# Graph attention in two layers: where an attention block's output projection stands in the order of work

## The chip, the cores and the metric

The kernel runs on one core of one Trainium2 chip. The metric is device time in microseconds (us) of one execution, lower is better. Five engines run their own instruction queues beside each other: PE (TensorE, the matmuls), DVE (VectorE), ACT (ScalarE), POOL (GpSimd) and SP (SyncE, which here issues the DMAs). They wait for one another through semaphores.

## What is computed

The input is x of 8 elements, 2048 nodes and 256 features, with one adjacency matrix of 2048 x 2048 for all elements. Everything is in 32-bit floats. Two layers follow each other, cut here to what matters:

```
# layer 0: masked attention, 4 heads of 64, softmax apart over each chunk of 256 keys
scores = clip(q @ k.T / 8, -10, 10);  scores[adj == 0] = -10
attn   = softmax over the 256 keys of each of 8 chunks
ctx    = sum over chunks of attn @ v
out    = ctx @ Wo.T + bo + x
x      = layernorm(x + (layernorm(out) * gamma + beta))
# layer 1: graph attention
Wh     = x @ W;  e = leaky_relu(Wh @ a1 (rows) + Wh @ a2 (columns));  e[not adj] = -inf
h      = elu(softmax(e) @ Wh)
x      = layernorm(x + h)
```

## The kernel before, in words

Layer 0 works in blocks of 512 queries, named (b,ib): element b of 8, block ib of 4. A block passes over 8 chunks of 256 keys. Each chunk takes two **beats**, so there are 512 beats with attention in them, and a block has 16. The order of all instructions is written out by hand, and each engine executes its own in that order.

One beat, in the order in which it is written:

1. `begin_beat` (lines 816 to 834), for layer 1: exponentials of the edge weights that are ready (`weights`, ACT, with a sum on POOL), the next edge steps' linear part (`low`, ACT, line 714), and `leaky` on DVE (line 718) for the steps begun in the beat before.
2. Scores: four matmuls of 512 columns on PE (line 899) into two tiles of PSUM, two clips and caps on DVE (line 909), two exponentials on ACT (line 912).
3. `middle_of_beat` (line 914): `edges`, the masks of layer 1, on DVE (line 723).
4. Values of the chunk before (line 928). In the first beat of a chunk, which is even, two parts: the denominators (part 2) and the first half of the values (part 0). In the second beat, which is odd, the other half (part 1). Each part takes one PSUM tile of the pool `ps_m`, which has two buffers, and ACT copies it out (lines 936 and 942).
5. `end_beat` (lines 842 to 856): the products of layer 1 on PE (line 746), then one step of each generator in `ahead` (the preludes of layer 1) and `fins` (projections of keys and values, the block ends, and so on), then what is due in `agenda`, such as the scaling of a chunk's values and its addition to the context `ctxT` (DVE line 963, POOL line 964).

Layer 1 may begin an edge step 1.5 times per beat, which gives two and one in turn. A step passes `low`, `leaky` and `edges`, then `weights` and its product two beats after it began.

The generator `fin` (line 343) ends a block of layer 0. It loads x, prepares `y` = x + bo on POOL, and waits until the last chunk has been added to `ctxT`. It goes on in the beat after that, which is an odd one. Then, in one beat, it writes the output projection (two tiles `po` of pool `ps_m`, 8 matmuls in all at line 357, each added to `y` on DVE at line 364) and the statistics of the first normalization. In the following beats come the normalization (ACT), gamma and beta (POOL), the statistics of the second one, its normalization with the store `h_d` and the count `fin_near`, and the transposes `pt` (line 383) with the store `hT_d`. The prelude of element b in layer 1 begins when `fin_near` shows all four blocks; it makes Wh (`pw`), the masked maxima (`fb`, line 438), the rows `pab` (line 461), and then layer 1's steps can begin. All of `po`, `pt`, `pw`, `pab`, and the projections `pq`, `pk`, `pv` share the two buffers of `ps_m` with the values.

The first product of a layer-1 block writes the one PSUM tile `us`, which ACT must have copied out for the block before it (line 773).

Of the kernel before, what the change touches and what calls it, by code (L numbers as in the profile page):

```python
# [9 lines left out]
F32 = mybir.dt.float32  # L10
# [9 lines left out]
P = 128  # L20
# [8 lines left out]
def tile_adj_attention__then__gat(  # L29
# [35 lines left out]
    nc = tc.nc  # L65
    B, N, F = x.shape
    H, D = 4, 64
    CHUNK = 256
    KC = F // P
    NT = N // P  # L70
    IB = 512
    NIB = N // IB
    TPB = IB // P
# [12 lines left out]
    ps_m = ctx.enter_context(tc.tile_pool(name="ps_m", bufs=2, space=PSUM))  # L86
# [21 lines left out]
    def load_w(name, w):  # L108
        t = const.tile([P, KC, F], F32, name=f"WT_{name}")
        nc.sync.dma_start(out=t, in_=w.rearrange("(k p) o -> p k o", p=P))  # L110
        return t
# [11 lines left out]
    WT = {"k": load_w("k", WkT)}  # L123
# [187 lines left out]
    def stats(src, name):  # L311

        st = two.tile([P, TPB, 6], F32, tag="st", name=f"st_{name}")
        mv = two.tile([P, TPB, 2], F32, tag="mv", name=f"mv_{name}")
        for t in range(TPB):
            nc.vector.bn_stats(st[:, t, :], src[:, t, :])
            nc.vector.bn_aggr(mv[:, t, :], st[:, t, :])
            if t == TPB // 2 - 1 and beat < 2 * NIB * NCH:
                yield
        rstd = two.tile([P, TPB], F32, tag="rstd", name=f"rstd_{name}")  # L320
        nc.vector.tensor_scalar_add(rstd, mv[:, :, 1], EPS)
        nc.gpsimd.tensor_tensor(rstd, rstd, nhalf, ALU.pow)
        return mv, rstd

    def normalize(dst, mv, rstd, name):
        nmr = two.tile([P, TPB], F32, tag="nmr", name=f"nmr_{name}")
        nc.vector.scalar_tensor_tensor(nmr, mv[:, :, 0], -1.0, rstd, ALU.mult, ALU.mult)
        for t in range(TPB):
            nc.scalar.activation(
                dst[:, t, :], dst[:, t, :], AF.Identity, bias=nmr[:, t : t + 1], scale=rstd[:, t : t + 1]  # L330
            )

    def bc_rows(v):
        return v.unsqueeze(1).to_broadcast([P, TPB, F])
# [2 lines left out]
    hT_d = dram.tile([B, NIB, P, KC, IB], F32, name="hT_d")  # L337
    fin_near = [0] * B
    ctx_done = {}
    fins = []  # L340

    def fin(b, ib, ctxT):


        xt = one.tile([P, TPB, F], F32, tag="x", name=f"x{b}_{ib}")
        nc.sync.dma_start(out=xt, in_=x[b, ts(ib, IB), :].rearrange("(t p) f -> p t f", p=P))
        yield
        y = one.tile([P, TPB, F], F32, tag="y", name=f"y{b}_{ib}")
        nc.gpsimd.tensor_add(y, xt, bc_rows(bo_bc))  # L349
        nc.gpsimd.tensor_add(xt, xt, bc_rows(beta_bc))  # L350
        while (b, ib) not in ctx_done or ctx_done[b, ib] == beat:
            yield
        for t2 in range(TPB // 2):
            po = ps_m.tile([P, 2, F], F32, tag="m", name=f"po{b}_{ib}_{t2}")
            for j in range(2):
                for k in range(KC):
                    nc.tensor.matmul(  # L357
                        po[:, j, :],
                        ctxT[:, k, ts(2 * t2 + j, P)],
                        WT["o"][:, k, :],  # L360
                        start=(k == 0),
                        stop=(k == KC - 1),
                    )
            nc.vector.tensor_add(y[:, ts(t2, 2), :], po, y[:, ts(t2, 2), :])
        mv, rstd = yield from stats(y, f"a{b}_{ib}")
        yield
        normalize(y, mv, rstd, f"a{b}_{ib}")
        yield
        engine = nc.vector if (b, ib) == (B - 1, NIB - 1) else nc.gpsimd
        engine.tensor_mul(y, y, bc_rows(gamma_bc))  # L370
        engine.tensor_add(y, y, xt)
        yield
        mv, rstd = yield from stats(y, f"b{b}_{ib}")
        yield
        normalize(y, mv, rstd, f"b{b}_{ib}")
        nc.sync.dma_start(out=h_d[b, ib], in_=y)
        fin_near[b] += 1
        yield
        hT = four.tile([P, KC, IB], F32, tag="xT", name=f"hT{b}_{ib}")
        for k in range(KC):  # L380
            pt = ps_m.tile([P, TPB, P], F32, tag="m", name=f"pt{b}_{ib}_{k}")
            for t in range(TPB):
                nc.tensor.transpose(pt[:, t, :], y[:, t, ts(k, P)], ident)
            nc.scalar.copy(hT[:, k, :], pt.rearrange("p t c -> p (t c)"))
        if (b, ib) == (B - 1, NIB - 1):
            states[b]["hT"] = hT
        else:
            nc.sync.dma_start(out=hT_d[b, ib], in_=hT)
# [447 lines left out]
    def middle_of_beat():  # L836
        nonlocal edged
        for s in leaking:
            s.edges()
        edged = leaking  # L840
# [32 lines left out]
    for J in range(total + 1):  # L873
        b, ib, j = J // (NIB * NCH), J // NCH % NIB, J % NCH
        live = J < total
        if live and j == 0:
            ctxT = one.tile([P, 2, IB], F32, tag="ctx", name=f"ctxT{b}_{ib}")
        cur = {"b": b, "ib": ib, "j": j, "es": [], "ctxT": ctxT, "v": vs[min(b, B - 1)], "name": f"{b}_{ib}_{j}"}
        for half in range(2):
# [14 lines left out]
            if live:  # L894
                scs = []
                for hp in range(NPAIR):
                    sc = ps_s.tile([P, 2, IB], F32, tag="sc", name=f"sc{b}_{ib}_{c}_{hp}")
                    for h in range(2):
# [4 lines left out]
                            start=True,  # L903
                            stop=True,
# [5 lines left out]
                for hp in range(NPAIR):  # L910
                    e = eight.tile([P, 2, IB], F32, tag="e", name=f"e{b}_{ib}_{c}_{hp}")
                    nc.scalar.activation(e, scs[hp], AF.Exp)  # L912
                    cur["es"].append(e)
            middle_of_beat()

            early = J < NIB * NCH
            if prev is not None:
                if half == 0:

                    pool, tag = (one, "hr") if early and J % 3 == 2 else (two, "un")  # L920
                    prev["un"] = pool.tile([P, 2, IB], F32, tag=tag, name=f"un{prev['name']}")
                for part in ((2, 0), (1,))[half]:
                    m = ps_m.tile([P, IB], F32, tag="m", name=f"u{prev['name']}_{part}")
                    for i in range(2):
                        pc = 2 * prev["j"] + i
                        for h in range(H):
# [5 lines left out]
                                start=(i == 0),  # L932
                                stop=(i == 1),
# [3 lines left out]
                    else:  # L937
# [20 lines left out]
                        def scaled(p=prev):  # L958
                            r2 = p["r"].unsqueeze(1).to_broadcast([P, 2, IB])
                            if p["j"] == 0:  # L960
                                nc.vector.tensor_mul(p["ctxT"], p["un"], r2)
                            else:
                                nc.vector.tensor_mul(p["un"], p["un"], r2)  # L963
                                nc.gpsimd.tensor_add(p["ctxT"], p["ctxT"], p["un"])  # L964
                            if p["j"] == NCH - 1:
                                ctx_done[p["b"], p["ib"]] = beat
                            if p["j"] == NCH - 3:
                                fins.append(fin(p["b"], p["ib"], p["ctxT"]))
# [66 lines left out]
```

## Time and profile before

| what | value |
|---|---|
| time, median of 3 runs | 4400.04 us (4389.66 to 4401.98) |
| the profiled execution's own time | 4387.29 us |
| its span | 4385.5 us |
| mean granted clock of TensorE | 0.98 |
| DVE, scores clipped, L909 | 1024 x 1223 ns |
| PE, scores, L899 | 4096 records, 1060.4 us |
| PE, values and denominators, L928 | 980.9 and 497.5 us |
| PE, products of layer 1, L746 | 878.6 us |
| PE, output projection, L357 | 512 records, 120.2 us |
| DVE, sum of projection and y, L364 | 64 x 689 ns |

Each program matmul in 32-bit floats shows as two or four records. In the lines of groups, waits and timelines, `a<-b` reads "writes a from b", L is the line of the kernel, and the bracket at the end of a timeline line is the time that the engine stood idle before it, with what ended the wait. PEld is the load of weights into PE, which overlaps matmuls.

### The profile page before, as it was taken

What the parts mean: (1) busy time and instruction counts of PE and PEld (TensorE: products, weight loads), DVE (VectorE), ACT (ScalarE), POOL (GpSimd) and SP (SyncE); (2) the same over time, 40 slices, a digit from 0 to 9 for tenths busy, and PEclk for the clock granted to TensorE, in tenths of its full rate; (3) what the DMA queues carried; (4) which work ended last, traced back from release to release, by engine and by line L of the source; (5) the groups of instructions that cost most, each with busy time, mean ns of one, the idle gap of its engine ahead of it and who ended that gap; (6) DMA issues with size and microseconds to landing.
All of it is one profiled execution on the core that took longest, in us unless ns stands there. A gap on an engine that the chain in (4) does not pass through costs nothing. (4 is left out here: it accounts for less than half of the span.)

```text
span 4385.5 us, 61171 instructions
## 1 busy us (share of the span) xinstructions
PE 4064.2 (93%) x23053; PEld 1907.6 (43%) x23053; DVE 3417.7 (78%) x4530; ACT 2564.4 (58%) x3842; POOL 1760.5 (40%) x901
## 2 busy tenths in 40 slices
PE   8889989999999999999899999999999999899767
PEld 3223334454344534454344543445434454344456
DVE  5876589965998669976699766996579965888777
ACT  5655556665566556666566665566556665555546
POOL 0222235543455334444245442554325542354420
PEclk9999999999999999999999999999999999999889
DMA  5554232222332233321333223232232222322321
GB/s 166 182 163 149 71 115 86 83 73 89 99 90 81 64 107 102 100 75 51 105 102 98 74 74 105 85 95 78 70 106 85 89 78 67 115 83 80 123 73 58
DMA packets 257641, 415.63 MB, mean 95 GB/s; under 512 B 85440, under 2 KB 120512, under 8 KB 256448
## 3 DMA queue, kind: packets, MB, share of 16 engines
q1 hardware_dynamic: 257344, 411.71, 30.5%
q8 instruction: 181, 2.97, 0.3%
q14 instruction: 116, 0.95, 0.1%
HBM read 340.66 MB, written 68.88 MB: 93 GB/s over the span
## 5 line engine op out<-in xcount | busy, mean ns | idle before, releaser
L912 ACT ACTIVATE e<-sc 128x1024 f32<-128x1024 f32 x1024 | 1034.2, 1020 | 1049.9 <-DVE sc L909 1006.7
L909 DVE SCALAR_TENSOR_TENSOR sc<-sc,mk 128x1024 f32<-128x1024 f32 x1024 | 1206.7, 1223 | 538.3 <-PE sc L899 352.6
L899 PE MATMUL sc<-qT,kT 64*128 64x512 f32 x4096 | 1060.4, 633 | 86.7 <-ACT e L912 86.2
L964 POOL TENSOR_TENSOR ctxT<-ctxT,un 128x1024 f32<-128x1024 f32 x224 | 568.5, 2538 | 1145.3 <-DVE un L963 1007.0
L928 PE MATMUL u<-e,v 128*32 128x512 f32 x8192 | 980.9, 597 | 0.0
L746 PE MATMUL us<-wh,w 128*128 128x256 f32 x3584 | 878.6, 395 | 81.9 <-ACT w L727 60.4
L746 PEld LDWEIGHTS us<-wh,w 128*128 128x128 f32 x3584 | 667.7, 193 | 422.2 <-ACT w L727 110.7
L736 POOL TENSOR_TENSOR acc<-acc,w 128x512 f32<-128x512 f32 x392 | 601.7, 1535 | 544.9 <-ACT w L727 534.4
L899 PEld LDWEIGHTS sc<-qT,kT 64*128 64x128 f32 x4096 | 347.2, 189 | 611.6 <-ACT e L912 281.8
L718 DVE SCALAR_TENSOR_TENSOR w<-ab,sj,w 128x512 f32<-128x512 f32 x512 | 571.5, 1137 | 4.6 <-ACT w L714 4.5
L928 PEld LDWEIGHTS u<-e,v 128*32 128x32 f32 x8192 | 240.6, 110 | 659.7 <-issue 543.9
L928 PE MATMUL u<-e,ones 128*32 128x512 f32 x4096 | 497.5, 604 | 0.0
L723 DVE TENSOR_TENSOR w<-w,mk 128x512 f32<-128x512 f32 x512 | 458.6, 917 | 37.1 <-DMA mk<-mask 34.6
L438 DVE CUSTOM_DVE_ANT_0 fb<-sj_row,fb 128x1024 bf16<-128x1024 f32 x240 | 387.8, 1626 | 2.3 <-DMA fb<-far 2.3
L714 ACT ACTIVATE w<-ab,sj 128x512 f32<-128x512 f32 x512 | 352.2, 714 | 8.7 <-POOL acc L734 5.4
L727 ACT ACTIVATE w<-w 128x512 f32<-128x512 f32 x512 | 308.8, 629 | 75.9 <-DVE w L723 75.3
L936 ACT COPY un<-u 128x512 f32<-128x512 f32 x512 | 300.5, 587 | 66.5 <-PE u L928 57.6
L963 DVE TENSOR_TENSOR un<-un,r 128x1024 f32<-128x1024 f32 x224 | 278.1, 1242 | 42.2 <-DMA r<-rd 36.7
L928 PEld LDWEIGHTS u<-e,ones 128*32 128x32 f32 x4096 | 107.8, 110 | 356.5 <-issue 305.4
L950 DVE RECIPROCAL dc<-dc 128x16 f32<-128x16 f32 x256 | 63.9, 249 | 149.8 <-DMA dc<-ds 134.0
L942 ACT COPY ds<-u 128x512 f32<-128x512 f32 x256 | 148.5, 580 | 3.0 <-PE u L928 2.5
L349 POOL TENSOR_TENSOR y<-x,bo_bc 128x1024 f32<-128x1024 f32 x32 | 77.6, 2426 | 163.6 <-DMA x<-in_x_dram 103.0
(112 smaller groups left out, 3114.7 us busy)
## 6 DMA issues: line engine op xcount, KB each, us to landing
r<-rd SPq DMA_DIRECT2D x256, 256.0 KB
mk<-mask SPq DMA_DIRECT2D x120, 512.0 KB
fb<-far SPq DMA_DIRECT2D x240, 256.0 KB
xT_k<-in_xT_dram SPq DMA_DIRECT2D x32, 512.0 KB
raw<-in_adjT_dram SPq DMA_DIRECT2D x32, 512.0 KB
rawf<-in_adj_dram SPq DMA_DIRECT2D x32, 512.0 KB
x<-in_x_dram SPq DMA_DIRECT2D x32, 512.0 KB
h_d<-y SPq DMA_DIRECT2D x32, 512.0 KB
```

Source lines behind the costliest of these rows:

```text
L438: nc.vector.tensor_tensor_reduce(out=fb, in0=row, in1=fb, scale=1.0, scalar=2 * FAR * 0.999, op0=ALU.add, op1=ALU.max, accum_out=dst,)
L714: nc.scalar.activation(self.w, k["ab"][:, 1, :], AF.Identity, bias=k["sj"][:, 1, c : c + 1])
L718: nc.vector.scalar_tensor_tensor(self.w, k["ab"][:, 0, :], k["sj"][:, 0, c : c + 1], self.w, ALU.add, ALU.max)
L723: nc.vector.tensor_tensor(self.w, self.w, self.k["mks"][self.c // HT][:, self.c % HT, :], ALU.min)
L727: nc.scalar.activation(self.w, self.w, AF.Exp)
L736: nc.gpsimd.tensor_add(k["acc"], k["acc"], self.w)
L746: nc.tensor.matmul(k["us"][:, t, :], self.w[:, ts(t, P)], k["wh"][c // TPB][:, c % TPB, 0:F], start=(first and t % 2 == 0), stop=last, ski ...
L899: nc.tensor.matmul(sc[:, h, :], kTs[b][c // TPB][h * D : (h + 1) * D, hp, ts(c % TPB, P)], qT[h * D : (h + 1) * D, hp, :], start=True, sto ...
L909: nc.vector.scalar_tensor_tensor(scs[hp], scs[hp], -CLIP, cap, ALU.max, ALU.min)
L912: nc.scalar.activation(e, scs[hp], AF.Exp)
L928: nc.tensor.matmul(m[h * DH : (h + 1) * DH, :], prev["v"][pc // TPB][:, pc % TPB, f0 : f0 + DH] if part < 2 else ones[:, 0:DH], prev["es"] ...
L964: nc.gpsimd.tensor_add(p["ctxT"], p["ctxT"], p["un"])
```

## The change

The projection's code becomes a function. For all blocks but the last of the last two elements, (6,3) and (7,3), `fin` puts that function into a list, and the list is emptied in the next beat's middle: after the scores and `edges` of that beat, and before its values. For those two blocks it is called at once, as before. `fin` yields after having put it there, so what follows in `fin`, from the statistics on, is written one beat later for the 30 blocks.

```diff
@@ -337,6 +337,7 @@
     ctx_done = {}
+    middle = []
     fins = []
@@ -350,18 +351,27 @@
         while (b, ib) not in ctx_done or ctx_done[b, ib] == beat:
             yield
-        for t2 in range(TPB // 2):
-            po = ps_m.tile([P, 2, F], F32, tag="m", name=f"po{b}_{ib}_{t2}")
...
-            nc.vector.tensor_add(y[:, ts(t2, 2), :], po, y[:, ts(t2, 2), :])
+
+        def output_projection():
+            for t2 in range(TPB // 2):
+                po = ps_m.tile([P, 2, F], F32, tag="m", name=f"po{b}_{ib}_{t2}")
+                for j in range(2):
+                    for k in range(KC):
+                        nc.tensor.matmul(
+                            po[:, j, :],
+                            ctxT[:, k, ts(2 * t2 + j, P)],
+                            WT["o"][:, k, :],
+                            start=(k == 0),
+                            stop=(k == KC - 1),
+                        )
+                nc.vector.tensor_add(y[:, ts(t2, 2), :], po, y[:, ts(t2, 2), :])
+
+        if b < B - 2 or ib < NIB - 1:
+            middle.append(output_projection)
+            yield
+        else:
+            output_projection()
         mv, rstd = yield from stats(y, f"a{b}_{ib}")
@@ -912,6 +922,8 @@
             middle_of_beat()
+            while middle:
+                middle.pop(0)()
```

More of the change, by code (lines that the diff above doesn't have):

```diff
@@ L352, in fin @@
             yield
-        for t2 in range(TPB // 2):
-            po = ps_m.tile([P, 2, F], F32, tag="m", name=f"po{b}_{ib}_{t2}")
[L355 to L364, printed above, removed]
+        def output_projection():
[16 more added lines that the diff above has]
+            output_projection()
         mv, rstd = yield from stats(y, f"a{b}_{ib}")
```

## The prediction

> **What bounds the kernel now.** Read in this order: busy times, who PE waited for, the output projection's tile `po`, then the timelines of PE and DVE around one projection. The waits' columns are total us, times, longest.
>
> ```profile
> PE 4064.2 (93%) x23053; PEld 1907.6 (43%) x23053; DVE 3417.7 (78%) x4530; ACT 2564.4 (58%) x3842; POOL 1760.5 (40%) x901
> ...
> PE sc L899 <- ACT e L912: 86.2, 57, 6.3
> PE us L746 <- ACT w L727: 60.4, 43, 10.8
> PE us L746 <- ACT hx L773: 21.5, 7, 3.9
> PE po L357 <- POOL ctxT L964: 16.4, 13, 2.6
> PE pab L461 <- ACT ds L942: 16.2, 18, 1.8
> ...
> PE pt L383 <- ACT ds L942: 14.4, 13, 1.8
> ...
>   DVE y L364: 61.8, 35
> ```
>
> PE is busy for 93% of the span. By windows, 82 us of its idle time lie after the last scores (276.7 less 195.1 busy from 4108.8 on); before, it idles some 25 us per element of attention (526.8 less 502.5 from 1084.6 to 1611.4), in short gaps. So a stall put into PE's order counts, and a gap filled counts. The last line says that DVE waits 61.8 us for `po`. That is mostly harmless, because DVE has slack in most stages. Block (2,1), PE first and then DVE:
>
> ```profile
> 1222.43 3.72 PE L746 MATMUL us<-wh,w 128*128 128x256 f32 x16
> 1225.99 3.61 PE L357 MATMUL po<-WT_o,ctxT 128*128 128x256 f32 x16
> 1229.53 1.99 PE L899 MATMUL sc<-qT,kT 64*128 64x512 f32 x8
> 1231.45 1.92 PE L928 MATMUL u<-e,ones 128*32 128x512 f32 x16
> 1233.19 1.90 PE L928 MATMUL u<-e,v 128*32 128x512 f32 x16
> ...
> 1246.28 2.43 PE L746 MATMUL us<-wh,w 128*128 128x256 f32 x8 [2.94 <-ACT hx L773]
> ```
> ```profile
> 1220.91 2.81 DVE L718 SCALAR_TENSOR_TENSOR w<-ab,sj,w 128x512 f32<-128x512 f32 x1
> 1223.65 2.35 DVE L909 SCALAR_TENSOR_TENSOR sc<-sc,mk 128x1024 f32<-128x1024 f32 x2
> 1225.91 0.84 DVE L723 TENSOR_TENSOR w<-w,mk 128x512 f32<-128x512 f32 x1
> 1226.68 1.21 DVE L438 CUSTOM_DVE_ANT_0 fb<-sj_row,fb 128x1024 bf16<-128x1024 f32 x1
> ...
> 1227.91 0.69 DVE L364 TENSOR_TENSOR y<-po,y 128x512 f32<-128x512 f32 x1
> 1229.64 0.69 DVE L364 TENSOR_TENSOR y<-po,y 128x512 f32<-128x512 f32 x1 [1.03 <-PE po L357]
> ...
> 1232.57 1.41 DVE L718 SCALAR_TENSOR_TENSOR w<-ab,sj,w 128x512 f32<-128x512 f32 x2
> 1233.90 2.36 DVE L909 SCALAR_TENSOR_TENSOR sc<-sc,mk 128x1024 f32<-128x1024 f32 x2
> ```
>
> PE runs without a gap here, and DVE is behind: it clips the scores of this beat 3 to 5 us after PE began them.
>
> **What the Trainium skill says.** "PSUM — Partial Sum Buffer", Engine vs sequencer instructions: the queues of ScalarE, VectorE and GpSimdE are strictly first in, first out, and matmuls complete in program order. The trace agrees: the second y above waits 1.03 us and everything of the next beat on DVE comes after it. "Perfetto Trace Analysis", Matmuls: independent groups should rotate through PSUM banks so that evacuating one overlaps the next. Here the pool `m` has two buffers for u, po, pk, pv, pw, pt and pab alike, and the pt and pab rows above are waits for a buffer of it. "SBUF — State Buffer", Who interferes with whom: a DVE instruction with two SBUF inputs contends with a GpSimd one that reads SBUF. L718 takes 0.66 us alone and 2.81 us above, so a DVE queue time has an error of some 2 us.
>
> **The change, part by part.** Call T the odd beat at whose end the projection stands now. It moves into beat T+1, after that beat's scores and before its values. No instruction is added: 16 po matmul records (3.6 to 3.7 us) and two y adds (1.4 us) per block, 30 of 32 blocks. No DMA is issued by the moved part itself. Everything after it in `fin` (bn statistics, both normalizations, gamma and beta, h_d store, transposes pt, hT_d store) comes one beat later, so these two stores stand one beat later on SP's queue. The h_d store then precedes an even beat's rd and r issues, where today the hT_d store does: an exchange, cost nothing; r is used two beats (about 15 us) after. Without that cover it costs the 2 us of one normalization.
>
> The new wait: values part 2 takes the buffer of po0, so it needs the first y add, which on DVE now stands behind leaky, two clips and edges of T+1. Behind the waiting matmul on PE stand all values and layer-1 products.
>
> A second consequence follows from the code. fin of (b,3), b up to 5, ends one beat later; the prelude of layer 1 waits for it, so layer 1 of elements 0 to 5 starts one beat later (beat T+23 of that block, not T+22). Layer 1 alternates two steps and one step per beat; starting on an even beat it is turned over: the beat with both value parts (3.7 us of u) now also gets two products (3.7 us), the odd one (1.9 us of u) gets one (2.0 us). PE's pair of beats stays at 4.0 + 5.6 + 5.6 = 15.2 us; DVE's too.
>
> Sums, against the profiled execution (span 4385.5, run 4387.3; the median of the runs shown is 4400.0, 0.3% above it):
>
> 1. Element 0 (no layer 1). (0,0) and (0,1) are DVE-bound; y waits of about 1.0 and 1.5 us go. (0,2): PE has no gap, 0. (0,3): PE stands 2.63 us before po; scores need only exp of T, some 2.3 us earlier than ctxT, then po, then values find y ready: 1.9 us. Sum -4.4.
> 2. (b,0), seven blocks: DVE-bound. The y wait of 0.84 us shrinks to about 0.3: -0.5 each, -3.5. The gap before po (1.87 us in (2,0)) doesn't go: scores of T+1 need exp of T, which is as late.
> 3. (b,1), b = 1 to 6. In (2,1), turned over, PE reaches the end of T's products at 1226.4, ends scores at 1228.4 and po at 1232.0. DVE, with leaky x2 (3.6 with one held up), ends T at 1228.0, then leaky 0.7, clips 2.35, edges 0.75, first y 0.7: 1232.6. Stall 0.6 us; with (7,1) about +4. If T's second leaky is held up too, 2 us more each.
> 4. (b,2), b = 1 to 6. fin1's statistics (2.3 us) now lie at T; DVE ends T at 1366.8, first y at 1371.4, po ended at 1369.1: stall 2.3. The gap of 1.3 for ctxT goes, because scores come first and ctxT is long done. +1.0 each, with (7,2) +6.5.
> 5. (b,3): DVE is idle 4.7 us there, y is ready before po ends: 0.
> 6. The first product of a new layer-1 block waits for the copy of `us` (the 2.94 us line; 21.5 us in 7). It moves from T+2 to T+3, behind 3.7 us of values and not 1.9, so about 1.3 remains: -1.6 x 6 = -9.6.
> 7. pt (14.4 us) waits for the ds copy, because it follows parts 2 and 0 of an even beat. One beat later it follows part 1 alone, whose buffer before last is long free. A quarter kept: -11.
> 8. pab in the same way, 0.42 and 0.90 us in each of six elements: -7.8.
>
> Total -25.8. Against that stands what the turn-over does in the 43 layer-1 beats of six elements, which no row shows. Between none of it and +35 us (a wait of the 0.34 or 0.56 us kind, L746 for L727, in half of the beats, less those that vanish). I take +8: where ACT and DVE are late, about a third of what PE recovers returns as another wait. Net -18 us: 4369 for the profiled execution, 4382 on the scale of the median. After the last scores nothing moves, since (6,3) and (7,3) are excepted.
>
> **Rivals.**
> - A, forecast, 0.57: short PE gaps close, 4382. For it: items 6 to 8 are repeated at the same place in each element.
> - B, given back, 0.18: the closed gaps return a beat later as waits for exp or for the new y, and only items 1 and 2 stay, 4400 - 4 = 4396. For it: DVE is idle only 5.3 us of the 135.9 in the window 1196.3 to 1332.2, which follows (2,1), so PE can't run ahead of it. Against it: at pt and pab the buffers are late on account of ACT's order, not of DVE's load.
> - C, slower, 0.25: values stall on the first y. It decides from where DVE gets to that add more than about 2 us after po ends on average. Were the turn-over not there, T+1 would have two leaky and two edges and (b,2) the maxima (3 us) before it: I get 2.1 us for (b,1) and 4.2 - 1.4 = 2.8 for (b,2), seven blocks each, 34 us; with one more hold-up of 2 us in half of these blocks 48, less items 1, 2 and half of 7 and 8: about +25, 4425 us. For it: 2.81 us leaky lines just at this place. Against it: DVE idle in (b,3) and no layer 1 in (b,0).
> - That nothing changes in the order is excluded: 30 blocks take the new branch.
>
> **How the numbers follow.** 4382 is A's. A's own range is 4355 to 4392, C reaches to 4440. From 4350 to 4420 about a tenth is left out at either end. About 0.3% (13 us) can be told from no change: A gives mostly faster, B same, C slower; 0.58, 0.17, 0.25.
>
> **What would show it.** Step 3 and 4: a new row, PE u waiting for DVE y, of 10 to 25 us in total. Over 50 us is C. Step 6: the hx row falls from 21.5 to about 12. Steps 7 and 8: the pt row near 4, pab near 8. Step 1: the po row for ctxT nearly gone in element 0. The turn-over: beats in (b,2) alternate about 9.4 and 5.9 us in place of 7.4 each; if they don't, the step on the prelude is wrong. The sc row for exp should stay near 86; if it grows by over 20, DVE is the bound and B or C holds.

## The result and the profile after

The changed kernel takes 4549.44 us (median of 4 runs, 4547.73 to 4553.29). The kernel before, measured beside it, takes 4399.95 us. The ratio is 1.0349, with a 95% interval of 1.0337 to 1.0362: slower by some 150 us, where the prediction said 18 us faster and a range up to 4420.

The profiled execution took 4548.56 us. Its span is 4546.7 us, 161.2 us longer than before, and its mean granted clock is 0.963 where it was 0.980. The busy times, from the page of the changed kernel:

```profile
PE 4131.4 (91%) x23053; PEld 1925.3 (42%) x23053; DVE 3493.0 (77%) x4530; ACT 2575.6 (57%) x3842; POOL 1761.9 (39%) x901
```

The same number of instructions keeps PE busy 67 us longer, and PE idles 94 us more (span less busy: 415.3 after, 321.3 before). The two add up to the 161 us. There are two things to explain: new gaps, and slower matmuls. In the lines below, `sc` are the scores, `e` their exponentials, `u` a chunk's values or denominators in PSUM, `un` and `ds` their copies, `w` the edge weights of layer 1, `us` its products and `hx` the copy of these. `dc`, `rd` and `r` are the denominators on their way: inverted, written to DRAM by one DMA, and spread over the partitions by the next. What PE waited for, from the view of its waits (total us, times, longest):

```profile
PE sc L909 <- ACT e L922: 179.2, 76, 6.3
PE us L756 <- ACT w L737: 56.1, 31, 10.8
PE pt L393 <- ACT un L948: 51.3, 23, 4.8
PE pw L408 <- ACT un L948: 21.9, 14, 4.9
PE u L940 <- DVE y L367: 19.2, 13, 1.6
...
PE us L756 <- ACT hx L783: 10.5, 7, 3.9
```

Scores now wait 93 us longer for exponentials (86.2 before), the transposes `pt` 37 us longer (14.4 before, for `ds`). The wait that the change was sure to add, values for the first add to `y`, is 19.2 us. The rows of `po` for `ctxT` (16.4) and of `pab` for `ds` (16.2) are gone.

The slower matmuls come with the gaps. Here are two places in the changed kernel's PE timeline, around scores that follow a gap (columns: start, length, operation, records, and in the bracket the idle time before):

```profile
1136.44 1.99 PE L909 MATMUL sc<-qT,kT 64*128 64x512 f32 x8
1138.36 1.92 PE L940 MATMUL u<-e,v 128*32 128x512 f32 x16
1145.76 3.52 PE L909 MATMUL sc<-qT,kT 64*128 64x512 f32 x8 [5.48 <-ACT e L922]
...
1067.29 1.11 PE L393 MATMUL pt<-ident,y 128*128 128x128 f32 x4 [2.87 <-ACT un L948]
1068.33 2.98 PE L909 MATMUL sc<-qT,kT 64*128 64x512 f32 x8
```

The same eight records take 1.99 us in a run without gaps, and 3.52 or 2.98 us behind a gap. The view by stretches of time shows why (second column the length, PEclk the one before the last two):

```profile
1142.00:1145.70 3.70, 0.00 (x0) 0.00 (x0) 3.58 (x5) 1.02 (x1) 2.34 (x1) 0.97 0.14 42
1145.70:1149.20 3.50, 3.44 (x8) 1.13 (x8) 3.50 (x6) 1.50 (x3) 0.00 (x0) 0.55 0.40 133
1149.20:1152.60 3.40, 3.40 (x18) 2.96 (x16) 1.93 (x2) 2.05 (x2) 0.00 (x0) 1.00 0.38 99
```

Behind the gap the granted clock is 0.55 for about 3.5 us and then full again. Summed over the clock records of the trace, TensorE stood at half clock for 342 us in 63 spells, against 180 us in 34 spells before; gaps of PE over 2 us number 61, and 37 before. Of 162 us more at half clock at most half is lost work, 81 us, which covers the 67. With the slower matmuls, the 94 us of gaps come to 161.

By block, as time from first scores to first scores of the next block: in elements 1 to 6 the (b,0) cost 36.0 us more in sum, the (b,1) 35.5, the (b,2) 47.6, the (b,3) 45.9. Element 0 costs 3.1 more, element 7 7.0 less. Layer 1 of an element runs beside the attention of the next one. The loss is thus spread over all of the time in which layer 1 runs, and is missing where there is none (element 0) or where it starts on its old beat (that of element 6, beside element 7).

### The profile page after: what moved, and what is told of

It is laid out like the page before. It is cut to its first block, busy times and chain, and to the rows that moved or that the text cites. A ratio compares the mean times of both kernels' runs of the same rounds, so it can differ in the third digit from the quotient of the medians.

```text
span 4546.7 us, 61091 instructions
## 1 busy us (share of the span) xinstructions
PE 4131.4 (91%) x23053; PEld 1925.3 (42%) x23053; DVE 3493.0 (77%) x4530; ACT 2575.6 (57%) x3842; POOL 1761.9 (39%) x901
## 5 line engine op out<-in xcount | busy, mean ns | idle before, releaser
L909 PE MATMUL sc<-qT,kT 64*128 64x512 f32 x4096 | 1105.8, 656 | 179.8 <-ACT e L922 179.2
L746 POOL TENSOR_TENSOR acc<-acc,w 128x512 f32<-128x512 f32 x392 | 583.6, 1489 | 724.3 <-ACT w L737 714.6
L909 PEld LDWEIGHTS sc<-qT,kT 64*128 64x128 f32 x4096 | 360.6, 195 | 725.2 <-ACT e L922 358.3
L728 DVE SCALAR_TENSOR_TENSOR w<-ab,sj,w 128x512 f32<-128x512 f32 x512 | 655.7, 1301 | 6.2 <-ACT w L724 6.1
L940 PE MATMUL u<-e,ones 128*32 128x512 f32 x4096 | 508.1, 615 | 19.2 <-DVE y L367 19.2
L733 DVE TENSOR_TENSOR w<-w,mk 128x512 f32<-128x512 f32 x512 | 417.5, 836 | 8.3 <-DMA mk<-mask 5.7
L975 DVE TENSOR_TENSOR un<-un,r 128x1024 f32<-128x1024 f32 x224 | 352.8, 1575 | 44.5 <-DMA r<-rd 44.3
L724 ACT ACTIVATE w<-ab,sj 128x512 f32<-128x512 f32 x512 | 352.3, 713 | 51.3 <-PE us L756 40.0
L448 DVE CUSTOM_DVE_ANT_0 fb<-sj_row,fb 128x1024 bf16<-128x1024 f32 x240 | 337.5, 1417 | 4.3 <-DMA fb<-far 4.1
L322 POOL TENSOR_TENSOR rstd_a<-rstd_a,nhalf 128x4 f32<-128x4 f32 x32 | 57.7, 1804 | 281.1 <-DVE rstd_a L321 218.2
```

The source lines that it names most:

```text
L448: nc.vector.tensor_tensor_reduce(out=fb, in0=row, in1=fb, scale=1.0, scalar=2 * FAR * 0.999, op0=ALU.add, op1=ALU.max, accum_out=dst,)
L724: nc.scalar.activation(self.w, k["ab"][:, 1, :], AF.Identity, bias=k["sj"][:, 1, c : c + 1])
L728: nc.vector.scalar_tensor_tensor(self.w, k["ab"][:, 0, :], k["sj"][:, 0, c : c + 1], self.w, ALU.add, ALU.max)
L733: nc.vector.tensor_tensor(self.w, self.w, self.k["mks"][self.c // HT][:, self.c % HT, :], ALU.min)
L746: nc.gpsimd.tensor_add(k["acc"], k["acc"], self.w)
L909: nc.tensor.matmul(sc[:, h, :], kTs[b][c // TPB][h * D : (h + 1) * D, hp, ts(c % TPB, P)], qT[h * D : (h + 1) * D, hp, :], start=True, sto ...
```

## The experiments

Each ratio is to the kernel before, run beside it on the same chip (medians 4389.2 to 4397.9 us in the five groups); 1% is 44 us. "Moved" means the projection in the middle of the next beat. e2 to e7, e9 to e11 and e14 to e16 ran twice each, the other experiments six times or more. The third and fourth columns say how many beats later than before layer 1's prelude and its steps are written, in elements 0 to 5.

| run | projection | prelude | steps | leaky | time us | ratio, 95% interval |
|---|---|---|---|---|---|---|
| the change | moved | +1 | +1 | ahead of clips | 4549.4 | 1.0349 [1.0337, 1.0362] |
| e1 | moved but for all (b,3) | 0 | 0 | ahead | 4413.3 | 1.0044 [1.0030, 1.0058] |
| e2 | old place | +1 | +1 | ahead | 4545.6 | 1.0349 [1.0324, 1.0374] |
| e3 | moved | 0 | 0 | ahead | 4436.6 | 1.0101 [1.0075, 1.0126] |
| e4 | old place, statistics a beat later | +1 | +1 | ahead | 4530.5 | 1.0314 [1.0289, 1.0339] |
| e5 | old place | +2 | +2 | ahead | 4474.8 | 1.0190 [1.0164, 1.0215] |
| e6 | old place | 0 | +1 | ahead | 4496.0 | 1.0238 [1.0218, 1.0258] |
| e7 | old place | +1 | +2 | ahead | 4435.7 | 1.0101 [1.0082, 1.0119] |
| e8 | moved in element 7 alone | 0 | 0 | ahead | 4383.6 | 0.9981 [0.9973, 0.9989] |
| e9 | moved | +1 | +1 | ahead | 4554.1 | 1.0376 [1.0331, 1.0420] |
| e10 | old place | 0 | +1 | ahead | 4486.7 | 1.0222 [1.0178, 1.0266] |
| e11 | moved | +1 | +1 | ahead | 4562.9 | 1.0396 [1.0351, 1.0441] |
| e12 | old place | 0 | +1 | behind clips | 4389.8 | 0.9989 [0.9980, 0.9998] |
| e13 | old place | 0 | 0 | behind | 4388.6 | 0.9990 [0.9982, 0.9998] |
| e14 | moved | +1 | +1 | behind | 4502.2 | 1.0246 [1.0205, 1.0288] |
| e15 | old place | +1 | +1 | behind | 4463.6 | 1.0155 [1.0117, 1.0193] |
| e16 | moved | 0 | +1 | behind | 4441.1 | 1.0104 [1.0061, 1.0146] |

### Is it the projection's place, or layer 1's later start? (e1 to e4)

Two theories stood after the first reading: the projection itself disturbs its beat (values behind the first `y` add, everything after it a beat late), or layer 1, which starts one beat later because `fin_near` is counted later, meets the attention's fixed work in another phase. e1 leaves the last block of every element in the old place, so that layer 1 keeps its beats:

```diff
-        if b < B - 2 or ib < NIB - 1:
+        if ib < NIB - 1:
```

> The change with (b,3) of every element left in its old place, so that 24 blocks are moved and layer 1 starts on the same beats as in the kernel before. Theory P (what costs is that layer 1 and its prelude start one beat later, on beats of the other parity): 4385 to 4430 us, half-clock time near the 180 us of before. Rival M (what costs is the moved projection itself, or the later rest of its block): about 24/30 of the loss stays, 4520 us. Rival V (values stall on the first y): loss in the rows of PE u waiting for DVE y, which would grow as T+1 has two leaky again, over 40 us in total.

e2 is the kernel before with nothing but one more `yield` ahead of the prelude:

```diff
+        if b < B - 2:
+            yield
```

> The kernel before, with one yield more in the prelude of layer 1 of elements 0 to 5; no projection is moved. Theory P: most of the loss without any moved projection, 4490 to 4550 us, and the clip of scores waiting on the spread of r as in the change. Rival M: 4400 us within 15.

e3 is the change with one `yield` less in the prelude, which puts layer 1 back on its beats:

```diff
-        yield
+        if b >= B - 2:
+            yield
```

> The change in full, with one yield fewer in the prelude of elements 0 to 5, so that layer 1 starts on the beats of the kernel before. Theory P: 4385 to 4430 us. Rival M: 4540 us, as the change.

e4 leaves the projection in its place and puts the extra `yield` of the 30 blocks behind it, ahead of the statistics:

```diff
             nc.vector.tensor_add(y[:, ts(t2, 2), :], po, y[:, ts(t2, 2), :])
+        if b < B - 2 or ib < NIB - 1:
+            yield
```

> The kernel before with the projection in its old place, but the rest of each block's end (statistics on) one beat later, for the 30 blocks. It keeps the later chain and the later start of layer 1, and drops the new place of the matmuls. Theory P, and a theory C (the later chain of each block costs): 4500 to 4560 us, as the change. If the place of the matmuls is what costs: 4400 to 4420.

e2 alone gives the whole ratio, 1.0349, without a moved projection. e1 and e3, with the projection moved and layer 1 on its old beats, cost 0.4 and 1.0%. e4, projection in the old place, costs 3.1%. So the later start of layer 1 is enough for the loss. The moved projection, with the end of its block a beat later, is a smaller loss by itself (44 us in e3), and it adds nothing to be seen when the other is there. By block, e3 loses most of it in (b,0), 25 us, where the transposes `pt`, a part of the later end, wait 22 us for `un`, and in (b,3), 20 us, where the values wait 21 us for `y` (sums over elements 1 to 6).

### The steps or the prelude, and does the phase come round? (e5 to e8)

e5 has two more `yield` ahead of the prelude in place of e2's one: layer 1 then has its two-step beats where they were, even or odd.

> The kernel before, with two yields more in the prelude of elements 0 to 5: layer 1 starts two beats later, on beats of the old parity. Theory P1 (parity): 4385 to 4415 us. Theory P2 (lateness, a beat of layer 1 is lost per element and has to be made up): at least the 150 us of the run with one yield, 4540 us or more.

e6 leaves the prelude on its beat and starts only the steps one beat later. e7 has e2's `yield` and this edit together: the prelude is one beat later and the steps two, so that beats with two steps are even or odd as before.

```diff
-            st["ab"][ib] = (beat + 2, query_bc(ab_d, f"{b}_{ib}"))
+            st["ab"][ib] = (beat + 2 + (b < B - 2), query_bc(ab_d, f"{b}_{ib}"))
```

> The kernel before, with the edge steps of layer 1 of elements 0 to 5 started one beat later by their due beat alone; the prelude's own work stays on its beats. Theory S (two products in the beat of two value parts, and what waits with them, cost): 4480 to 4545 us. Theory W (the prelude's own work, its loads, maxima and pw on beats of the other parity, costs): 4390 to 4415 us.

> The kernel before, with the prelude of elements 0 to 5 one beat later and the steps two beats later, so that the steps keep their parity and only the prelude's own work is turned over. Theory S: 4390 to 4420 us. Theory W: 4480 to 4545 us. If both have a share, this run's loss and that of the steps alone add up to about 150 us.

e8 moves the projection in element 7 alone, where the row by row comparison showed a gain:

```diff
-        if b < B - 2 or ib < NIB - 1:
+        if b == B - 1 and ib < NIB - 1:
```

> Only the three moved blocks of element 7, (7,0) to (7,2). In the run that keeps (b,3) the rows of element 7 are 13.5 us shorter than before, from gaps of PE that close. If these are worth their face: 4379 us against 4392, ratio 0.997. If they come from the earlier elements' shifted state: 1.000.

e6, with the steps alone later by one, gives 2.38%, some 105 us. What e2 has above it, 1.11% or some 49 us, is the prelude's beat. e7 says the same in another way, if steps two beats later cost nothing: with the two-step beats back on the old side it costs 1.01%, 44 us. Two causes, then: the steps, some 105 us, and the prelude, some 45. e5 has the old side too and is still 1.9% slower, with the prelude two beats later, so to keep the side isn't enough; e5 differs from e7 in the prelude's beat alone. e8 beats the kernel before by 0.19% [0.11, 0.27], where 0.3% were expected.

### Two explanations that fell (e9 to e11)

In the changed kernel the prelude's row of 1 MB, `sj_row`, is issued just ahead of a chunk's `rd` and `r`. The SP queue and DVE there:

```profile
1128.91 0.34 SPq L431 DMA_DIRECT2D sj_row<-sj_d  x1
1129.30 0.90 SPq L440 DMA_DIRECT2D fb<-far  x2
1130.24 0.68 SPq L964 DMA_DIRECT2D rd<-dc  x1
1135.55 0.55 SPq L968 DMA_DIRECT2D r<-rd  x1
```
```profile
1141.93 1.23 DVE L975 TENSOR_TENSOR un<-un,r 128x1024 f32<-128x1024 f32 x1 [5.01 <-DMA r<-rd]
1143.27 0.25 DVE L962 RECIPROCAL dc<-dc 128x16 f32<-128x16 f32 x1
1143.44 2.34 DVE L919 SCALAR_TENSOR_TENSOR sc<-sc,mk 128x1024 f32<-128x1024 f32 x2
```

`r` is issued 5.3 us behind `rd`, where the next pair (1143.55 and 1144.96) has 1.4. DVE stands 5.01 us for `r`, the clips behind it are late, and this ends as the 5.48 us gap at 1145.76. In the kernel before, the row was issued at 1083.60, behind an `r` at 1078.57 and well ahead of the next `rd` at 1091.94; the first maximum that reads it came 10.5 us later and didn't wait. e9 puts the row behind the pair:

```diff
+        def broadcast():
+            nc.sync.dma_start(out=row, in_=sj_d.rearrange("r c -> (r c)").partition_broadcast(P))
...
+            at(beat, broadcast)
```

> The change in full, with the prelude's 1 MB broadcast of sj_row issued behind that beat's rd and r on SP's queue and not ahead of them (elements 0 to 5). Theory: rd takes 5 us from issue to the issue of r once per element because the broadcast and two fb loads stand in front; DVE then stands 5.0 us for r and PE 5.5 us for exp, and a spell of half clock follows. If so, that gap goes in six elements: 33 us and up to 2 us of clock each, 4505 to 4520 us. If the place on the queue is not the cause: 4549.

It gains nothing. `r` now comes 2.6 us behind `rd`, but the maxima of the prelude need the row itself, and stand on DVE ahead of the next clips. DVE and PE of e9:

```profile
1138.46 1.23 DVE L454 CUSTOM_DVE_ANT_0 fb<-sj_row,fb 128x1024 bf16<-128x1024 f32 x1 [6.58 <-DMA sj_row<-sj_d]
```
```profile
1144.37 3.79 PE L915 MATMUL sc<-qT,kT 64*128 64x512 f32 x8 [6.85 <-ACT e L928]
```

In either order DVE stops for 5 to 6.6 us here, once for `r` and once for the row itself. The order of the two issues wasn't the cause.

For the steps, S1 in the expectations is that the beats of PE become unequal (9.1 and 5.7 us), so that in the short one DVE and ACT can't follow; S2 is that DVE or ACT is late for another reason. e10 is e6 with the second product of an even beat put off to the next one, which makes PE's beats equal again (7.4 us where nothing stops them); e11 puts the edits of e9 and e10 into the change.

```diff
+        due = carried + weighted
+        carried = []
+        if beat % 2 == 0 and len(due) == 2 and due[1].k["b"] < B - 2:
+            carried = [due.pop()]
-        for s in weighted:
+        for s in due:
```

> The run with the steps of layer 1 one beat later, and in it the second of two products of an even beat is put off to the end of the next, odd beat, so that PE has one product in the beat of two value parts and two in the other, as in the kernel before; leaky, edges and exponentials stay turned over. Theory S1 (the short odd beats of PE make it come to the scores before exp has freed their tiles): most of the 105 us comes back, 4390 to 4430 us, and PE's waits for exp fall from 141 to under 105. Theory S2 (the turned-over work on DVE and ACT is what costs): 4480 to 4500.

> The change in full with both: the broadcast behind rd and r, and the second product put off. If these two are the main ways in which the later layer 1 costs, what is left is the moved projection and the rest of the prelude: 4430 to 4460 us. If the put-off products help only by chance in the other order: 4500 or more.

e10 is at 2.22% against e6's 2.38%, the intervals overlap, and the change with both edits isn't faster either. As the main cause S1 fell.

### What the later steps do: `leaky` ahead of the clips (e12 to e14)

This is e6 on DVE, in two beats of (2,2) in which two edge steps are due, and PE and POOL beside them:

```profile
1302.18 4.06 DVE L718 SCALAR_TENSOR_TENSOR w<-ab,sj,w 128x512 f32<-128x512 f32 x2
1306.17 2.35 DVE L909 SCALAR_TENSOR_TENSOR sc<-sc,mk 128x1024 f32<-128x1024 f32 x2
...
1319.31 3.95 DVE L718 SCALAR_TENSOR_TENSOR w<-ab,sj,w 128x512 f32<-128x512 f32 x2
1323.19 2.35 DVE L909 SCALAR_TENSOR_TENSOR sc<-sc,mk 128x1024 f32<-128x1024 f32 x2
```
```profile
1308.50 2.26 PE L899 MATMUL sc<-qT,kT 64*128 64x512 f32 x8 [1.47 <-ACT e L912]
...
1325.52 2.26 PE L899 MATMUL sc<-qT,kT 64*128 64x512 f32 x8 [1.73 <-ACT e L912]
```
```profile
1302.87 2.83 POOL L964 TENSOR_TENSOR ctxT<-ctxT,un 128x1024 f32<-128x1024 f32 x1
1305.66 1.72 POOL L736 TENSOR_TENSOR acc<-acc,w 128x512 f32<-128x512 f32 x1
...
1318.67 2.37 POOL L964 TENSOR_TENSOR ctxT<-ctxT,un 128x1024 f32<-128x1024 f32 x1 [1.23 <-DVE un L963]
```

Two `leaky` take about 4 us, at the head of an odd beat, just while POOL adds `un` to `ctxT`. The clips stand behind them, so the exponentials are late and PE stops at the next scores. In the kernel before the two stood in an even beat and took 1.41 and 2.41 us:

```profile
1285.80 1.41 DVE L718 SCALAR_TENSOR_TENSOR w<-ab,sj,w 128x512 f32<-128x512 f32 x2
1287.12 2.36 DVE L909 SCALAR_TENSOR_TENSOR sc<-sc,mk 128x1024 f32<-128x1024 f32 x2
...
1299.32 2.41 DVE L718 SCALAR_TENSOR_TENSOR w<-ab,sj,w 128x512 f32<-128x512 f32 x2
```

The Trainium skill, "SBUF — State Buffer", Who interferes with whom, has the rule for it: a DVE instruction with two SBUF inputs contends with a GpSimd one that reads SBUF. `leaky` has two, and the sum over the 512 of them rises from 571.5 us (mean 1137 ns) before to 655.7 us (1301 ns) in the change. S3 in the expectations is this theory. The edit takes `leaky` out of the clips' way:

```diff
     def begin_beat(rate):
...
-        for s in leaking:
-            s.leaky()
     def middle_of_beat():
         nonlocal edged
+        for s in leaking:
+            s.leaky()
         for s in leaking:
             s.edges()
```

e12 is e6 with it, e13 the kernel before with it, e14 the change with it.

> The run with the steps of layer 1 one beat later (4496 us), and with leaky of each beat behind the clips of that beat, no longer ahead of them. S3 (two leaky stand on DVE ahead of an odd beat's clips, beside the sums on POOL, take about 4 us where they took 1.4 to 2.4, and so the clips, the exponentials and the scores of the next even beat are late): the 105 us mostly go, 4390 to 4430 us, and the wait of scores for exp falls from 141 to under 100 us. If it is not leaky's place on DVE: 4480 to 4510 us. Numbers between would be a share of it.

> Control: the kernel before with leaky behind the clips. S3: little to win there, since the even beats' leaky take 1.4 to 2.4 us for two and one alone 0.7 to 2.8: 4370 to 4400 us. If this gains as much as the run beside it does, then leaky's place costs any order the same and is not what the later steps cost. Should edges come late for the exponentials of the weights, it is slower than 4400 us, with a larger wait of products for w.

> The change with leaky behind the clips. S3: 4549 us less some 70 to 100, since the prelude's one beat, about 45 us, stays: 4450 to 4480 us; clock spells at half rate fall from 342 us to about 280. If it is not leaky's place: 4535 to 4560 us.

e12 falls from 1.0238 to 0.9989: all of the steps' 105 us go. The wait of scores for exp goes with it; first e6, then e12:

```profile
PE sc L899 <- ACT e L912: 141.1, 83, 6.3
...
PE sc L899 <- ACT e L912: 90.1, 53, 6.3
```

The control e13 stays within 0.1% of the kernel before, so the edit is no general gain: it is worth nothing in the old order and 105 us in the order with later steps. That `leaky` ahead of the odd beats' clips is what the later steps cost is shown by this pair. That POOL is what makes it slow is not shown by a run: none took POOL's sums away. The traces fit it, instruction by instruction. In the kernel before, 198 of the 512 `leaky` have no TENSOR_TENSOR of POOL beside them, and none of these takes over 753 ns; the 302 that have one for more than half of their time take 1416 ns on average, up to 2884. In the change they are 172, again 753 ns at most, and 324 with 1628 ns. A long one is met by POOL more easily, so this alone doesn't prove the direction; for a much smaller operation of DVE, lines in the next section do.

In the change itself the edit gives back 47 us of 150, less than the 70 to 100 expected, and the half-clock time doesn't fall (349 us; 280 expected). By block, (b,2) is then as in e13 (5 us less in sum over six elements), but (b,0), (b,1) and (b,3) stay 31, 47 and 42 us above it.

### What is left: the prelude, and the `y` add (e15, e16)

e15 is e2 with `leaky` behind the clips, that is e14 with the projection in its old place. e16 is e14 with the prelude on its old beat and the steps one later (the edits of e3 and e6 together).

> The projection in its old place, layer 1 one beat later (the run of 4546 us), leaky behind the clips. If the parts add up, the steps' 105 us go and the prelude's 45 stay: 4425 to 4445 us; what the change with leaky behind the clips (4502 us) has above that, some 65 us, then belongs to the projection's own place in the new order of beats. If leaky's place gives back only the 47 us that it gave in the change: about 4500 us, and the projection's place costs nothing.

> The change with leaky behind the clips (4502 us) and the prelude back on its old beat, its steps kept one beat later. If the prelude's beat costs 45 us here too: 4450 to 4465 us, and the PE waits of 2.9 us for pt, 4.6 for pw and 5.2 us for scores, which stand at the prelude in each element, mostly go. What then stays above 4390 is the projection with its wait for y (42.7 us in the run before, at 6.6 us in each (b,3)). If the prelude's beat costs nothing here: 4490 to 4505 us.

The projection's old place, with the block's end on its old beats, takes 0.9% off e14 (1.0246 to 1.0155, 40 us), the prelude's old beat 1.4% (to 1.0104, 62 us). Together that is 102 of the 108 us that e14 lies above the kernel before. e15 misses its expected 4425 to 4445 by 19 us: against e12 the prelude's beat costs 1.7% there, 73 us, so its price lies between 45 and 73 us, by what else is in the order. By block, in sum over elements 1 to 6, this price lies mostly in (b,1): 44 us there and 2 in (b,0) between e14 and e16, 44 and 8 between e2 and e6. It is in (b,1) that DVE stops behind the 1 MB row; PE's wait for it, 5.20 us in (2,1) of e14, is 1.89 us in e16. All waits of scores for exponentials in (2,1) fall from 14.0 us to 8.2; among them is one of 3.12 us that is 0.25 in e16. Ahead of it two operations of the prelude on 128x4 stand on DVE beside POOL; DVE and then POOL of e14:

```profile
1155.95 2.22 DVE L464 TENSOR_TENSOR mx<-mx,sj 128x4 f32<-128x4 f32 x1
...
1158.41 2.22 DVE L466 TENSOR_TENSOR m<-sj,mx 128x4 f32<-128x4 f32 x1
```
```profile
1155.77 2.39 POOL L380 TENSOR_TENSOR y<-y,gamma_bc 128x1024 f32<-128x1024 f32 x1 [6.08 <-ACT y L329]
1158.23 2.37 POOL L381 TENSOR_TENSOR y<-y,x 128x1024 f32<-128x1024 f32 x1
```

In the kernel before, none of these operations takes over 165 ns. Here two in each of elements 1 to 6 take 2.2 us and end within 25 ns after POOL's, so it is DVE that is held up by POOL. The change has the same.

The row of `pw` for `un`, which stands in (b,0), is 27.9 us in e14 and 4.8 in e16, but its fall gains next to nothing there. The wait for `pt`, which the expectation put down to the prelude too, isn't: 29.4 us in e14 and 41.4 in e16.

The projection's part in e14 lies almost all in (b,3), where e14 is 35 us above e15. This wait comes there once in each of elements 1 to 6; PE and DVE of e14:

```profile
1397.02 3.72 PE L360 MATMUL po<-WT_o,ctxT 128*128 128x256 f32 x16
1407.35 3.64 PE L940 MATMUL u<-e,ones 128*32 128x512 f32 x16 [6.61 <-DVE y L367]
```
```profile
1394.75 2.64 DVE L728 SCALAR_TENSOR_TENSOR w<-ab,sj,w 128x512 f32<-128x512 f32 x2
1397.32 1.28 DVE L733 TENSOR_TENSOR w<-w,mk 128x512 f32<-128x512 f32 x2
1398.52 1.21 DVE L448 CUSTOM_DVE_ANT_0 fb<-sj_row,fb 128x1024 bf16<-128x1024 f32 x1
...
1402.00 2.36 DVE L919 SCALAR_TENSOR_TENSOR sc<-sc,mk 128x1024 f32<-128x1024 f32 x2
...
1406.61 1.27 DVE L367 TENSOR_TENSOR y<-po,y 128x512 f32<-128x512 f32 x2
```

Between 1399.7 and 1402.0 stand the statistics of `fin1`. PE has `po` done at 1400.7 and stands, because DVE reaches the `y` add only at 1406.6. In the change without the edit, the same place shows as 3.56 us at the scores and 1.58 us at the values: one lateness of DVE, met at another of PE's waits. So the row for `y` alone (19.2) doesn't show what the projection's place costs.

What e16 still loses against e13 lies in (b,3), 33 us, and in (b,0), 29 us, less 12 gained in (b,2). In (b,0) the transposes wait 17 us, where e13 has no such wait and e12 has 12; the rest of it stays open.

## Why the prediction was wrong, point by point

**The step that failed** is the one on the turn-over of layer 1: "Between none of it and +35 us ... I take +8". It saw that layer 1 starts one beat later, and which beats get two products, and priced it from PE's and DVE's sums ("PE's pair of beats stays at ... 15.2 us; DVE's too"). The beats are as it said, 9.1 and 5.7 us where nothing stops them in (2,2), for 9.4 and 5.9 predicted, and PE's sum over such a pair stays (14.8 us in both kernels). DVE's doesn't: it is busy for 75 us more in all. The later start alone costs 3.49% (e2), about 150 us, far above the bound of 35. What the sums don't hold is the order inside a beat: 105 us come from two `leaky` ahead of an odd beat's clips (e6 against e12), some 45 from the prelude's beat (e2 against e6, e7), most of it in (b,1), where DVE stops behind the row of 1 MB and beside POOL. The prediction looked at the line that shows it, 2.81 us for one `leaky` in an odd beat, and took it as an error of a queue time, not as a price that two `leaky` in each odd beat would then pay ahead of its clips.

**The clock** had no term. A gap was counted once, with its own length; here slower matmuls behind the gaps came on top, 67 us of 161. The Trainium skill, "TensorE: Matmul & The Clock Gate", Part 1, says that the clock halves after an idle window of about 3.4 us, which is free-running. The trace agrees in kind, since 60 of its 63 spells last 3.4 or 6.8 us, but less idle time was enough: 2.87 us at 1067.29 in the change, and 1.86 us in the kernel before, behind which the clock stood at half from 1124.8 on for 3.4 us.

**Step 7**, `pt` at -11 us, had the wrong sign: 14.4 us for `ds` became 51.3 us for `un`. It argued with one free buffer, "the buffer before last". But a transposition writes two tiles. The first four records found the free one; the other four need the tile of part 1, and its copy stands on ACT behind two exponentials. ACT of the changed kernel, beside the 2.87 us gap shown above:

```profile
1064.60 2.15 ACT L922 ACTIVATE e<-sc 128x1024 f32<-128x1024 f32 x2 [0.89 <-DVE sc L919]
1066.65 0.58 ACT L948 COPY un<-u 128x512 f32<-128x512 f32 x1
```

It is in e3 too (56.4 us, layer 1 on its old beats) and in e4 (60.6 us, the projection in its old place), so it belongs to the block's end coming a beat later.

**Step 6**, the `hx` row, was right in number (21.5 to 10.5; about 12 predicted), but its reason is only half of it. It was put down to the later start of layer 1, which brings the product behind 3.7 us of values and not 1.9. Later steps alone raise the row to 31.0, though (e6), since the exponentials ahead of the copy are late there; and the moved projection with layer 1 on its old beats gives 10.5 as well (e1, e3), since the copy then stands ahead of a normalization on ACT and not behind it. In the change both come a beat later, and the copy is behind that normalization as it was before (1238.70 and 1245.22 there):

```profile
1289.98 2.07 ACT L329 ACTIVATE y<-y,nmr_a,rstd_a 128x256 f32<-128x256 f32 x4 [0.91 <-DVE nmr_a L327]
...
1297.13 1.01 ACT L783 COPY hx<-us 128x1024 f32<-128x1024 f32 x1
```

Here PE does come later to the product, as the step said, and waits 1.10 us. So the reason fits the change, where the block's end and layer 1 move together; the later start alone doesn't shrink the wait.

**Steps 3 and 4**, the stall on the first `y`: the place was right, 1.54 to 1.61 us in elements 1 to 6 of the change. Predicted were 0.6 and 2.3. For (b,2) the 3.56 us at the scores of the same beat have to be added; the statistics of `fin1` were in the sum, two `leaky` of 3.67 us beside POOL weren't. Element 7, where a loss was expected too, gained 7.0 us. **Step 5** stands in the change: all 13 waits for `y` stand behind the projections of (b,1) and (b,2), none behind one of (b,3). **Step 8** came, and more: the `pab` row for `ds`, 16.2 us, is gone, where 7.8 were predicted. The later prelude does it in elements 1 to 6, as the step said (e2 keeps 3.3 us, all in element 7). But the row is gone in e1 and e3 too, with the prelude on its old beats, so the moved projection does it by a way of its own that wasn't followed. **Step 1** didn't come: the waits for `ctxT` went, but element 0 is 3.1 us longer and not 4.4 shorter. There `pt` waits 1.95 us in (0,1) and 1.96 us in (0,2), each with 6.8 us of half clock behind it, and these two blocks are 1.4 and 2.0 us longer. At the exchange of the two stores `r` is issued 3.2 us behind `rd` in (2,2) of the change (1322.53 and 1325.72), and DVE doesn't wait for it.

**Rivals.** The forecast's own test said that a growth of the scores' row by over 20 us means B or C. It grew by 93. C had the sign, but not the mechanism: values for `y` are 19.2 us, under its 50, and C's 4425 us is 124 short. None of the cases held the later start as a loss of its own.

## What to carry to other kernels

In an order that is written out by hand, moving one step by a beat moves everything that counts it; price first what starts later through a counter, and for it compare, beat by beat, which instructions now stand ahead of the critical one on each queue, since sums over a pair of beats don't show that. What is not needed in a beat goes behind what the critical engine waits for: with `leaky` behind the clips the later steps cost nothing (e12). Where a row of waits falls, undo the part that is thought to have done it before the reason is believed, and look for the same row where only another part was changed.

## What the runs showed of the hardware

- Half clock behind a gap: PE idle for 2.87 us is enough for eight score records to take 2.98 us and not 1.99; at one place in the kernel before, 1.86 us were enough. 60 of the 63 spells in the change last 3.4 or 6.8 us, and all of them 342 us.
- Two `leaky` of 128x512 with both inputs in SBUF take 1.41 us, and 3.7 to 4.1 us at the places shown, where POOL's adds run beside them; one takes at most 753 ns where POOL runs no TENSOR_TENSOR, and up to 2884 ns where it does. An operation on 128x4, at most 165 ns in the kernel before, took 2.22 us beside POOL's product in e14 and ended within 25 ns after it.
- Behind a broadcast of 1 MB and two loads of `fb`, the time from the issue of `rd` to that of `r` rose from 1.4 to 5.3 us, and with the row issued behind `r`, DVE waited 6.58 us for the row itself.
